# Two blocks of TensorE work moved ahead of the first flip of probabilities, in the local transformer of an adaLN network

## Chip, cores and metric

The kernel runs on one core of a Trainium2 chip. The metric is the time of one execution on the device in microseconds (us). Before the change the median of three runs is 4399.69 us (4398.7 to 4399.81).

## What is computed

The network has two layers, each with an attention part and a feed-forward part behind a modulated layer norm. Nearly all of the time goes into the feed-forward part of the first layer, which is itself a local transformer of six layers on 16 sequences of 256 tokens, width 128, with 16 heads of 64. Cut to what matters here, one of its layers is:

```python
def attn_layer(x, Wqkv, qs, ksc, Wo):
    q, k, v = jnp.split(x @ Wqkv, 3, -1)          # then split into heads
    q = l2norm(q) * qs
    k = l2norm(k) * ksc
    ...
    q = q * cos * scale + rotate_half(q) * sin * scale
    k = k * cos * inv + rotate_half(k) * sin * inv
    out = local_attention(q, k, v)                 # windows of 32 queries, 64 keys
    return out.transpose(0, 2, 1, 3).reshape(b, n, INNER) @ Wo

for i in range(DEPTH):
    x = attn_layer(shift_tokens(x), Wqkv[i], q_scale[i], k_scale[i], Wo[i]) + x
    x = ffn_layer(shift_tokens(x), ln_g[i], ln_b[i], W1[i], b1[i], W2[i], b2[i]) + x
```

`local_attention` multiplies each window of 32 queries with the 64 keys of its own and the preceding window, masks, takes a softmax, and multiplies with the values. `ffn_layer` is a layer norm, two matmuls with a gated GELU between them, and a matmul back.

## The kernel before

**Layout.** The state of two sequences (512 tokens) is one unit, kept as `z`, features on partitions. There are `NU = 8` units. A pair of heads fills 128 partitions, so a unit has `NP = 8` head pairs. Values and output projection are merged beforehand into one 128x128 matrix for each head (`wvo`), so that the "values" of the attention are the state itself.

**Steps.** The loop over `n` (lines 1009 to 1086) is one software pipeline over the six layers. A step takes two head pairs of one unit, `QS = 4` steps are a unit, 32 steps a layer, and 192 steps the stage, with nine more to drain. In one step stand stages of work of different head pairs:

- `project` (lines 633 to 661) multiplies the state with the weights of two head pairs (L648), squares the results on ScalarE (`sq`, L651), and forms the two halves of the rotary embedding on VectorE (L653, L656). The halves change places by DMA and are added by GpSimd one step later: four operations `rotate` (L664).
- `norms_sum` (lines 667 to 682), on even steps only, sums the squares of two steps over each head with the selector `sel`: 8 matmuls of 32 rows out (L672, 16 in the profile, which counts both passes of f32), and one copy `n2` on ScalarE (L681). `norms_inverse` turns the sums over and takes their inverse roots on GpSimd.
- `scaled` (L745) multiplies the keys with their inverse norms on GpSimd, twice in a step.
- `masked` (L771) writes the mask into two PSUM banks; `scores` (L793) adds 128 small products of queries and keys.
- `maxima` takes the row maxima `mx` (L805) and, in one small operation, the bias `nb` of the exponentials (L807), both on VectorE and once for each half `par` of the pair.
- `exponentials` (L815) are 16 activations on ScalarE for a step, in two groups of eight, `x = 0` and `x = 1`. The four operations `sq` of the same step's `project` stand between those of the first group: two exponentials, one `sq`, and so on. `divided` follows each group: a reciprocal (L828) and one product on GpSimd (`pr`, L830).
- `flipped` (L838), a step later, transposes the probabilities of one pair with four matmuls. The pair `x = 0` is copied out by ScalarE (L846), the pair `x = 1` by VectorE (L844), both into `prT`.
- `windows` (lines 747 to 764), on odd steps only, transposes the state of one sequence into the keys' view `xw`: eight matmuls (L755), one copy on ScalarE (L762), one on VectorE (L760), and one DMA that doubles it (L763).
- `weighted` (L856) multiplies state and probabilities, 8 matmuls (16 in the profile). In a step with `n % 4 == 0` it begins a unit and reads the `prT` that the two flips of the same step have just completed; in the other three it reads a `prT` completed earlier.
- `merging` (L877) multiplies with `wvo`, 32 matmuls in the profile. `ffn` is a generator that is advanced four times in a step.

With a unit of four steps, `ffn` always brings the same matmuls to the same place: the step with `n % 4 == 0` begins (after `merging`) with the last matmul of a unit's `ffn` (L962), the next with the variance (L912), the next with the gate (L939, GELU on ScalarE), and the last with the linear half (L949). Below they are called steps 0, 1, 2 and 3.

**What sets the order.** The region stands under a manual schedule for TensorE, VectorE, ScalarE and GpSimd: each executes its instructions in the order in which the Python code issues them. Four PSUM banks (`bank()`) are shared by everything but the scores and `merging`, each reused when its last reader is done.

Ahead of the change, the middle of a step is issued in this order:

```python
rotate(m, qs[m], got.pop(m))
...
flipped(p, 0, prs[n - 5], prTs[i, u])
...
    xws[v, s] = windows(v % NU, s)            # odd steps
sims = masked() if 0 <= n - 4 < N else None
...
flipped(p, 1, prs.pop(n - 5), prTs[i, u])
...
n2 = norms_sum([squares.pop(m) for m in range(2 * n - 4, 2 * n)])   # even steps
...
zxs[v, r] = weighted(r, xws[v, r // 2], prTs[v // NU, v % NU])
```

Of the kernel before, what the change touches and what calls it, by code (L numbers as in the profile page):

```python
# [19 lines left out]
NU = B // 2  # L20
U = 2 * L
DEPTH = 6
# [22 lines left out]
def adaln_kernel(  # L45
# [11 lines left out]
    def bank():  # L57
        return stage["ps"].tile([128, 512], F32, tag="mm", name="mm")

    def two(ap):  # L60
        return ap.rearrange("p (s t) -> p s t", s=2)
# [8 lines left out]
    def work(tag, shape=(128, 512), bufs=None):  # L70
        if stage.get("flat"):
            t = stage["flat"].tile([128, 512], F32, tag="flat", name=tag)
            if len(shape) == 4:
                t = t.rearrange("p (a b c) -> p a b c", a=shape[1], b=shape[2])
            return t
        kw = {} if bufs is None else {"bufs": bufs}
        return stage["pool"].tile(list(shape), F32, tag=tag, name=tag, **kw)
# [472 lines left out]
    with ExitStack() as es:  # L550
# [8 lines left out]
        def atile(tag, shape, bufs=None):  # L559
            kw = {} if bufs is None else {"bufs": bufs}  # L560
            return at.tile(list(shape), F32, tag=tag, name=tag, **kw)
# [29 lines left out]
        def load_ffn(i):  # L591
            w1 = wb.tile([128, 2 * FFH], F32, tag="w1", name="w1")
            nc.sync.dma_start(w1, io["L0_ffn_W1"][i])
            w2 = wb.tile([128, 3, D], F32, tag="w2", name="w2")
            nc.sync.dma_start(
                w2[:, 0:2, :],
                io["L0_ffn_W2"][i, 0:256, :].rearrange("(c k) d -> k c d", k=128),
            )
            nc.sync.dma_start(w2[0 : FFC[2], 2, :], io["L0_ffn_W2"][i, 256:FFH, :])
            return w1, w2  # L600
# [61 lines left out]
        def rotate(m, q, got):  # L662
            for j, r in enumerate((q, ks[m % 8][:, :, PAD:])):
                nc.gpsimd.tensor_tensor(r, r, two(got[:, j, :]), ALU.add)  # L664


        def norms_sum(squares):

            pn = bank()
            for odd in range(2):  # L670
                for g in range(4):
                    nc.tensor.matmul(  # L672
                        pn[32 * g : 32 * g + 32, :],
                        sel[:, odd, :],
                        squares[2 * (g % 2) + odd][1 - g // 2],
                        start=(odd == 0),
                        stop=(odd == 1),
                        skip_group_check=True,
                    )
            n2 = work("n2")  # L680
            nc.scalar.copy(n2, pn)  # L681
            return n2
# [59 lines left out]
        def scaled(m, kn):  # L742

            k = ks[m % 8][:, :, PAD:]
            nc.gpsimd.tensor_tensor(k, k, two(kn), ALU.mult)  # L745

        def windows(u, s):


            xw = atile("xw", (128, 8, 128))  # L750
            for g in range(2):
                pt = bank()
                for j in range(4):
                    w0 = 32 * (4 * g + j)
                    nc.tensor.transpose(  # L755
                        pt[0:64, j * 128 : (j + 1) * 128], zs[u][:, s, w0 : w0 + 64], ident
                    )
                dst = xw[0:64, 4 * g : 4 * g + 4, :].rearrange("p w d -> p (w d)")
                if g:
                    nc.vector.tensor_copy(dst, pt[0:64, :])  # L760
                else:
                    nc.scalar.copy(dst, pt[0:64, :])  # L762
            nc.sync.dma_start(xw[64:128], xw[0:64])  # L763
            return xw
# [207 lines left out]
        QS = NP // 2  # L972
        per = NU * QS
        N = DEPTH * per
# [3 lines left out]
        qs, squares, got, prs, prTs = {}, {}, {}, {}, {}  # L978
        xws, zxs, pys = {}, {}, {}
        inverses, kns = {}, {}  # L980
        n2 = rk = home = None
        behind, merges = [], []

        def place(n):

            return n // per, n % per // QS, 2 * (n % QS)
# [5 lines left out]
        def go_on(parts):  # L992
            for g in list(parts):
                if next(g, parts) is parts:
                    parts.remove(g)
# [12 lines left out]
        n = 0  # L1008
        while n < N + 9 or behind:
            layer, at_ = divmod(n, per)  # L1010
            if at_ == 13 and 0 < layer < DEPTH:
                wffs[layer] = load_ffn(layer)
            if 0 <= n - 4 < N:
                for m in (2 * (n - 4), 2 * (n - 4) + 1):
                    scaled(m, kns.pop(m))

            w, j = divmod(n - 9, QS)
            if 0 <= w < DEPTH * NU:
                if j == 0:
                    pys[w] = psy.tile([128, 512], F32, tag="y", name="y")  # L1020
                merging(j, zxs.pop((w, j)), vos[w // NU], pys[w])
                if j == QS - 1:
                    add_to_state(w % NU, pys.pop(w))
            if n % 2 and 3 <= n <= N + 1:
                home = norms_rows(rk)
            go_on(behind)
            go_on(merges)
            if 0 <= n - 1 < N:
                for m in (2 * (n - 1), 2 * (n - 1) + 1):
                    rotate(m, qs[m], got.pop(m))  # L1030
            if 0 <= n - 5 < N:
                i, u, p = place(n - 5)
                if p == 0:
                    prTs[i, u] = atile("prT", (128, NP, 512))
                flipped(p, 0, prs[n - 5], prTs[i, u])
            for s, lag in ((0, 7), (1, 9)):
                v, r = divmod(n - lag, QS)
                if r == 0 and 0 <= v < DEPTH * NU:
                    xws[v, s] = windows(v % NU, s)
            sims = masked() if 0 <= n - 4 < N else None  # L1040
            if 0 <= n - 5 < N:
                flipped(p, 1, prs.pop(n - 5), prTs[i, u])

            if n % 2 == 0 and 2 <= n <= N:
                n2 = norms_sum([squares.pop(m) for m in range(2 * n - 4, 2 * n)])
            v, r = divmod(n - 8, QS)
            if 0 <= v < DEPTH * NU:
                zxs[v, r] = weighted(r, xws[v, r // 2], prTs[v // NU, v % NU])
            go_on(behind)
            if sims:  # L1050
                m = 2 * (n - 4)
                rn = inverses[m // 4][:, m % 4 // 2]
                scores(sims, m, [qs.pop(m), qs.pop(m + 1)])
                pr = atile("pr", (128, 2, 4, 2, 64), 1)
                nbs = [maxima(sims[par], rn[:, par]) for par in range(2)]
                ssum = small("ssum", (128, 2, 4, 2))

            if n % 2 == 0 and 2 <= n <= N:
                rk, inverses[n // 2 - 1] = norms_inverse(n2)
            if 0 <= w < DEPTH * NU and j == QS - 1:  # L1060
                behind.append(ffn(w % NU, w // NU))
            go_on(behind)
            between = exponentials(0, sims, nbs, rn, pr, ssum) if sims else iter(())
            for m in (2 * n, 2 * n + 1):
                if n < N:
                    i, u, p = place(n)
                    qs[m], squares[m], got[m] = project(i, u, m, wqk[p + m % 2], between)
                if m % 2 == 0:
                    go_on(behind)
            if sims:  # L1070
                for x in range(2):
                    for _ in between:
                        pass
                    divided(pr[:, x], ssum[:, x])
                    between = exponentials(1, sims, nbs, rn, pr, ssum) if x == 0 else iter(())
                prs[n - 4] = pr
            if 0 <= n - 3 < N:
                for m in (2 * (n - 3), 2 * (n - 3) + 1):
                    kns[m] = widened(m, home)
            if layer + 1 < DEPTH:  # L1080
                if at_ == 18:
                    merges.append(merged(layer + 1))
                if at_ > per - QS:
                    p = 2 * (at_ - (per - QS) - 1)
                    wqk[p : p + 2] = [load_qk(layer + 1, p), load_qk(layer + 1, p + 1)]
            if at_ == 0 and 0 < layer < DEPTH:
                wqk[NP - 2 :] = [load_qk(layer, NP - 2), load_qk(layer, NP - 1)]
            n += 1
# [3 lines left out]
    for u in range(NU):  # L1092
        nc.sync.dma_start(xin[u], xhome[u])
        for hf in range(2):
            r, zv = zpart(u, hf)
# [13 lines left out]
    with ExitStack() as es:  # L1109
# [201 lines left out]
        N = len(steps)  # L1311
# [4 lines left out]
        n = 0  # L1316
        while n < N + 3 or running or merging:
# [12 lines left out]
            if n < N:  # L1330
                u, g, s, j = steps[n]
# [7 lines left out]
            if 0 <= n - 2 < N:  # L1339
                u, g, s, j = steps[n - 2]  # L1340
# [5 lines left out]
            if 0 <= n - 3 < N:  # L1346
                u, g, s, j = steps[n - 3]
# [116 lines left out]
```

## Time and profile before

One execution was profiled. It took 4399.63 us on the device, of which its span of instructions is 4397.6 us, with a mean granted TensorE clock of 0.964. The local transformer's pipeline runs from 396 us (its first waits) to 3765 us (its last `merging`).

| engine | busy in the span | us |
|---|---|---|
| TensorE, matmuls | 92% | 4060.0 |
| TensorE, weight loads | 60% | 2629.7 |
| VectorE | 64% | 2817.8 |
| ScalarE | 64% | 2829.9 |
| GpSimd | 59% | 2613.3 |

Four steps from the middle of the stage, each from the end of the last exponential of the step before to the end of its own, with the granted clock at 1.00 in each of the four windows:

| step | from, us | to, us | length, us | TensorE busy, us | ScalarE busy, us | GpSimd busy, us |
|---|---|---|---|---|---|---|
| 3 | 2007.30 | 2023.19 | 15.89 | 15.61 | 10.60 | 9.46 |
| 0 | 2023.19 | 2040.84 | 17.65 | 16.63 | 11.10 | 13.24 |
| 1 | 2040.84 | 2055.90 | 15.06 | 15.06 | 10.50 | 10.26 |
| 2 | 2055.90 | 2074.90 | 19.00 | 18.25 | 14.87 | 14.14 |

A timeline row gives the start, the duration, the engine (PE for matmuls, PEld for weight loads, DVE for VectorE, ACT for ScalarE, POOL for GpSimd), the line, the operation, the tiles it writes and reads, how many instructions are drawn together, and, in brackets, how long the engine was idle before it and what ended the wait. The ends of matmuls are modelled, so a busy TensorE is not one at its peak. In a group's row the first number behind the bar is the busy time in us, the second the mean of one in ns, and behind the second bar stands the idle time ahead of the group with those who ended it.

### The profile page before, as it was taken

The numbers are of one execution on the slowest core, as the hardware profiler recorded it, in microseconds if no ns is written. First come the engines' busy times: TensorE is split into PE (matmuls) and PEld (weight loads), VectorE is DVE, ScalarE is ACT, GpSimd is POOL, SyncE is SP. The second block draws the span as 40 slices with busy tenths as digits, with TensorE's granted clock in tenths as the row PEclk, the third lists the DMA queues.
The fourth block names the chain that finished last, engine by engine and source line by source line (L and its number), as shares of the span: only waits on it lengthen the run. The fifth ranks groups of instructions, "written<-read, shape, count | busy, mean of one in ns | idle before, by whom it ended". The sixth has DMA issues, their size and how long they took to land.

```text
span 4397.6 us, 118770 instructions
## 1 busy us (share of the span) xinstructions
PE 4060.0 (92%) x45721; PEld 2629.7 (60%) x45721; DVE 2817.8 (64%) x5987; ACT 2829.9 (64%) x9702; POOL 2613.3 (59%) x3302
## 2 busy tenths in 40 slices
PE   7667699999999999999999999999999998899998
PEld 4433466666666666666666666666666666545454
DVE  3434567777767777667676767767667675455554
ACT  3332567667676766767667676766767666477776
POOL 3323666676666676666766667666676764243432
PEclk7678899999999999999999999999999999999999
DMA  1022444444444444444444444444444442100000
GB/s 32 5 31 74 109 100 105 108 110 105 105 109 105 109 107 103 113 104 108 105 105 112 105 108 105 105 110 105 111 102 105 107 101 77 47 3 4 6 4 8
DMA packets 193548, 371.08 MB, mean 84 GB/s; under 512 B 42537, under 2 KB 83416, under 8 KB 192984
## 3 DMA queue, kind: packets, MB, share of 16 engines
q1 hardware_dynamic: 192984, 363.50, 33.5%
q8 instruction: 362, 5.93, 0.6%
q14 instruction: 202, 1.65, 0.1%
HBM read 127.92 MB, written 8.91 MB: 31 GB/s over the span
## 4 chain that ended last, share of the span: by engine, by line
PE 41%; DVE 20%; ACT 19%; POOL 5%; issue 5%; DMA 1%; SPq 0%; POOLq 0%; DVEq 0%; ACTq 0%
ACT pr L815 10%; PE mm L856 8%; PE sim L793 7%; DVE sent L653 5%; PE mm L672 4%; ACT sq L651 4%; PE mm L838 4%; POOL pr L830 4%; DVE k L656 3%; DVE q L656 3%; PE mm L648 3%; DVE mx L805 2%; PE mm L755 2%; PE mm L1251 2%; DVE nb L807 2%
## 5 line engine op out<-in xcount | busy, mean ns | idle before, releaser
L815 ACT ACTIVATE pr<-sim,nb,rq 128x64 f32<-128x64 f32 x3072 | 1229.5, 454 | 335.8 <-DVE nb L807 322.9
L830 POOL TENSOR_TENSOR pr<-pr,rsum 128x512 f32<-128x512 f32 x384 | 398.3, 1042 | 811.9 <-DVE rsum L828 776.8
L815 ACT ACTIVATION_READ_ACCUMULATOR pr<-sim,nb,rq 128x1 f32 x3072 | 784.9, 255 | 0.0
L877 PEld LDWEIGHTS y<-zx,wvo 128*128 128x128 f32 x6144 | 715.7, 192 | 91.5 <-issue 88.7
L877 PE MATMUL y<-zx,wvo 128*128 128x128 f32 x6144 | 717.5, 275 | 1.3 <-ACT zx L871 1.2
L648 PE MATMUL mm<-z,wqk 128*128 128x512 f32 x1536 | 705.1, 601 | 9.4 <-DMA wqk<-in_L_ffn_Wqkv_dram 7.2
L653 DVE SCALAR_TENSOR_TENSOR sent<-mm,vec,rope 128x512 f32<-128x512 f32 x768 | 569.9, 742 | 123.0 <-ACT sq L651 122.8
L651 ACT ACTIVATE sq<-mm 128x512 f32<-128x512 f32 x768 | 475.8, 620 | 33.6 <-PE mm L648 19.7
L664 POOL TENSOR_TENSOR k<-k,got 128x512 f32<-128x512 f32 x384 | 496.0, 1292 | 0.0
L664 POOL TENSOR_TENSOR q<-q,got 128x512 f32<-128x512 f32 x384 | 488.0, 1271 | 12.9 <-DMA got<-sent 9.8
L745 POOL TENSOR_TENSOR k<-k,kn 128x512 f32<-128x512 f32 x384 | 481.8, 1274 | 17.8 <-DMA kn<-rkh 17.8
L648 PEld LDWEIGHTS mm<-z,wqk 128*128 128x128 f32 x1536 | 278.7, 191 | 322.2 <-issue 236.4
L869 DVE COPY zx<-mm 128x512 f32<-128x512 f32 x384 | 265.4, 691 | 260.1 <-PE mm L856 260.0
L871 ACT COPY zx<-mm 128x512 f32<-128x512 f32 x384 | 224.8, 585 | 287.5 <-PE mm L856 287.5
L1224 POOL TENSOR_TENSOR pr<-pr,rsum 128x256 f32<-128x256 f32 (+1 forms) x256 | 206.1, 826 | 317.0 <-DVE rsum L1222 304.6
L856 PE MATMUL mm<-prT,xw 64*128 64x256 f32 x3072 | 390.0, 390 | 3.4 <-DVE zx L869 2.0
L805 DVE TENSOR_REDUCE mx<-sim 128x8 f32<-128x512 f32 x384 | 262.9, 685 | 172.3 <-PE sim L793 172.2
L856 PEld LDWEIGHTS mm<-prT,xw 64*128 64x128 f32 x3072 | 293.5, 187 | 122.3 <-issue 92.3
L838 PE MATMUL mm<-ident,pr 128*128 128x128 f32 x1536 | 245.3, 283 | 105.0 <-POOL pr L830 75.9
L838 PEld LDWEIGHTS mm<-ident,pr 128*128 128x128 f32 x1536 | 175.0, 142 | 270.1 <-POOL pr L830 240.6
L793 PEld LDWEIGHTS sim<-k,q 64*32 64x32 f32 x24576 | 265.7, 105 | 83.9 <-issue 56.8
L793 PE MATMUL sim<-k,q 64*32 64x64 f32 x24576 | 299.9, 226 | 16.6 <-issue 9.3
(236 smaller groups left out, 6649.2 us busy)
## 6 DMA issues: line engine op xcount, KB each, us to landing
got<-sent SPq DMA_DIRECT2D x1536, 128.0 KB
kn<-rkh SPq DMA_DIRECT2D x768, 128.0 KB
xw<-xw SPq DMA_DIRECT2D x96, 256.0 KB
wqk<-in_L_ffn_Wqkv_dram SPq DMA_DIRECT2D x48, 128.0 KB
bhome<-brow SPq DMA_DIRECT2D x1, 3072.0 KB
wv<-in_L_ffn_Wqkv_dram SPq DMA_DIRECT2D x12, 256.0 KB
wo<-in_L_ffn_Wo_dram SPq DMA_DIRECT2D x12, 256.0 KB
xt<-in_x_dram SPq DMA_DIRECT2D x8, 256.0 KB
```

Of the source, the lines that this page charges most:

```text
L648: nc.tensor.matmul(pp, wqk[:, j, :], xs, start=True, stop=True)
L651: nc.scalar.activation(sq, pp, AF.Square)
L653: nc.vector.scalar_tensor_tensor(two(sent[:, j, :]), two(pp), scale, tab[1], ALU.mult, ALU.mult)
L664: nc.gpsimd.tensor_tensor(r, r, two(got[:, j, :]), ALU.add)
L745: nc.gpsimd.tensor_tensor(k, k, two(kn), ALU.mult)
L793: nc.tensor.matmul(sims[par][32 * c : 32 * c + 32, c0 : c0 + 64], q[r, s, t0 : t0 + 32], k[r, s, t0 : t0 + 64], start=False, stop=True, sk ...
L805: nc.vector.tensor_reduce(mx, sim.rearrange("p (b k) -> p b k", b=8), AX.X, ALU.max)
L815: nc.scalar.activation(pr[:, x, st, par, :], sims[par][:, b * 64 : (b + 1) * 64], AF.Exp, bias=nbs[par][:, b : b + 1], scale=rn[:, par, b ...
L830: nc.gpsimd.tensor_tensor(prf, prf, rsum.unsqueeze(2).to_broadcast([128, 8, 64]), ALU.mult)
L838: nc.tensor.transpose(pt[:, st * 128 : (st + 1) * 128], pr[:, x, st].rearrange("p h k -> p (h k)"), ident,)
L856: nc.tensor.matmul(pz[par][:, w * 256 : (w + 1) * 256], xw[r, (2 * k + w) % 8, :], prT[r, :, 64 * k + 32 * w : 64 * k + 32 * w + 32], star ...
L877: nc.tensor.matmul(py[:, j * 128 : (j + 1) * 128], vo[:, h, :], zx[:, h % 2, h // 2, :], start=(h == 0), stop=(h == 2 * NP - 1), skip_grou ...
```

## The change

`norms_sum` (even steps) and `windows` (odd steps) are issued ahead of the first `flipped`, directly behind `rotate`, in place of behind the second and behind the first. Nothing is added or removed.

```diff
                 for m in (2 * (n - 1), 2 * (n - 1) + 1):
                     rotate(m, qs[m], got.pop(m))
+            if n % 2 == 0 and 2 <= n <= N:
+                n2 = norms_sum([squares.pop(m) for m in range(2 * n - 4, 2 * n)])
+            for s, lag in ((0, 7), (1, 9)):
+                v, r = divmod(n - lag, QS)
+                if r == 0 and 0 <= v < DEPTH * NU:
+                    xws[v, s] = windows(v % NU, s)
             if 0 <= n - 5 < N:
                 i, u, p = place(n - 5)
                 if p == 0:
                     prTs[i, u] = atile("prT", (128, NP, 512))
                 flipped(p, 0, prs[n - 5], prTs[i, u])
-            for s, lag in ((0, 7), (1, 9)):
-                v, r = divmod(n - lag, QS)
-                if r == 0 and 0 <= v < DEPTH * NU:
-                    xws[v, s] = windows(v % NU, s)
             sims = masked() if 0 <= n - 4 < N else None
             if 0 <= n - 5 < N:
                 flipped(p, 1, prs.pop(n - 5), prTs[i, u])
 
-            if n % 2 == 0 and 2 <= n <= N:
-                n2 = norms_sum([squares.pop(m) for m in range(2 * n - 4, 2 * n)])
             v, r = divmod(n - 8, QS)
```

In the built program the order on TensorE and ScalarE changes accordingly: in even steps L672 and its copy L681 now precede the first L838 and its copy L846, in odd steps L755 and its copy L762 do. The orders on VectorE and GpSimd are the same as before. The DMA queue of SyncE keeps its order but for the first few steps of the stage and one load of weights at each change of layer. PSUM banks are handed out in another order: in step 3 the first flip now takes the bank that the ScalarE copy of `windows` frees, and in step 2 the two flips take the first two banks that the GELU frees.

## The prediction

> **What bounds the kernel now.** I read the page first, then the waits of the flips (L838), then the timeline of four steps in a row, and last the operation `nb` (L807).
>
> ```profile
> PE 4060.0 (92%) x45721; PEld 2629.7 (60%) x45721; DVE 2817.8 (64%) x5987; ACT 2829.9 (64%) x9702; POOL 2613.3 (59%) x3302
> ...
> L838 PEld LDWEIGHTS mm<-ident,pr 128*128 128x128 f32 x1536 | 175.0, 142 | 270.1 <-POOL pr L830 240.6 <-POOL k L745 7.6 <-issue 5.2
> ```
>
> TensorE is the busiest engine, and its weight loads stand 240.6 us idle ahead of the flips until GpSimd has divided the probabilities. Together with the matmuls' own 75.9 us this is the gap that the moved work could fill. Whether filling it shortens a step depends on what starts the exponentials, since these are one unbroken chain on ScalarE: from the first to the end of the last 8.24 us in steps 1, 2 and 3 (2014.95 to 2023.19, for one) and 8.75 in step 0 (2032.09 to 2040.84).
>
> ```profile
> L807 DVE SCALAR_TENSOR_TENSOR nb<-mx,rq x384: 166/334/1308, 452.8 to 3718.5; 128x8 f32<-128x8 f32 x192
> ```
>
> This line of the view of `nb` (minimum, median, maximum in ns) shows an operation on 8 numbers a row that takes from 0.17 to 1.31 us. The timelines show why. Step 2:
>
> ```profile
> 2053.97 2.74 PE L939 MATMUL mm<-fx,w 128*128 128x512 f32 x6
> ...
> 2058.61 1.92 PE L672 MATMUL mm<-sq,sel 128*32 128x512 f32 x16
> ...
> 2063.98 1.26 POOL L664 TENSOR_TENSOR k<-k,got 128x512 f32<-128x512 f32 x1
> ...
> 2064.62 0.65 DVE L807 SCALAR_TENSOR_TENSOR nb<-mx,rq 128x8 f32<-128x8 f32 x1
> ...
> 2065.37 1.28 ACT L815 ACT_TABLE_LOAD   x1 [2.29 <-PE mm L648]
> ```
>
> `nb` begins at 2064.62 and ends at 2065.27, when the fourth rotation on GpSimd ends (2065.24). It is so in each of the four kinds of step: in step 0 it ends at 2031.97 and the rotation at 2031.95, in step 1 at 2047.55 and 2047.53, in step 3 at 2014.84 and 2014.81. The four rotations run without a gap, 1.24 us from one to the next, from a start that hangs on the exponentials before. So the next exponentials start on a grid of 1.24 us. TensorE decides only which tooth of it `nb` catches.
>
> **The even steps, step 2.** The block that moves is 16 matmuls. In issue it takes 1.85 us, from 2058.61 to the next matmul, L856, at 2060.46; the weights change from 128x32 to another split of the array, and each such change shows a pause of 0.09 us. Before, TensorE stood idle for most of the time between the end of L939 (its last issue at 2056.11, 0.43 for one of 512 columns, so 2056.54) and the sums. Now the sums start at 2056.54 + 0.09 = 2056.63, and the first flip at 2058.48; its probabilities have been ready since 2056.86, its bank (the first GELU) since 2057.83. From first flip to mask is 0.49 us (2056.91 to 2057.40), the mask 0.43, the second flip to `weighted` 0.53: `weighted` starts at 2059.94, against 2060.46. TensorE gains 0.52 us. The maxima, 3.43 us behind `weighted`, move along, and `nb` begins at 2064.10 in place of 2064.62. But the fourth rotation has started at 2063.98, 0.12 us earlier, and `nb` will end at 2065.27 as before. Gain: nothing.
>
> Here a rule and the trace are to be weighed. The Trainium skill, "Perfetto Trace Analysis", sections "Identifying the Most-Contended Engine" and "Optimization Strategy", says to find the gaps on the busiest engine and to make what they wait for come sooner. By it the 0.52 us would be gained, 40 times in the regular steps 2: 21 us. Another page, "SBUF — State Buffer", section "Who interferes with whom", speaks against: a VectorE operation with two SBUF inputs contends with a GpSimd operation that reads SBUF, and whichever comes second is fully blocked until the other ends. By that the gain is zero unless the start falls before 2063.98, and then 1.24 us at once. The ends of `nb` in all four steps are as the second rule has them, so I take zero.
>
> **Step 0.** Here the block was a cover.
>
> ```profile
> 2025.19 1.92 PE L672 MATMUL mm<-sq,sel 128*32 128x512 f32 x16
> ...
> 2026.25 0.69 DVE L844 COPY prT<-mm 128x512 f32<-128x512 f32 x1
> ...
> 2027.09 2.00 PE L856 MATMUL mm<-prT,xw 64*128 64x256 f32 x16
> ...
> 2031.25 0.72 DVE L807 SCALAR_TENSOR_TENSOR nb<-mx,rq 128x8 f32<-128x8 f32 x1
> ...
> 2031.78 3.60 PE L648 MATMUL mm<-z,wqk 128*128 128x512 f32 x8
> ...
> 2032.87 0.59 ACT L651 ACTIVATE sq<-mm 128x512 f32<-128x512 f32 x1
> ```
>
> `weighted` reads what the second flip has just delivered. The sums hid the copy of that flip (0.69 us, ended 2026.94) and were done at the same time as it. After the change nothing is between them. L962 gives TensorE free at 2023.33 in both versions (the idle time of TensorE ahead of both flips is only 0.24 us), so: sums at 2023.42, first flip 2025.27, mask 2025.76, second flip 2026.19, its copy 0.64 later (as 2042.42 to 2043.06 in step 1) at 2026.83 until 2027.52, `weighted` 0.12 to 0.15 later at 2027.67. That is 0.58 us late. VectorE is free for the copy (its work on `z` ends at 2026.22), so no more than that. From `weighted` on TensorE has no gap until `project` (L856, L793, L690, L903, L648), so all of it is 0.58 late.
>
> What waits for it: `nb` begins at 2031.83 and ends at 2032.00 (0.17 long, the rotation over at 2031.95), 0.03 us late, nearly free. The first exponentials are as good as on time. But the third operation on ScalarE is `sq` of the first product of `project`, whose second pass begins at 2032.21 and ends, with its modelled 0.59, at 2032.80; `sq` begins at 2032.87, with no slack. It now begins at 2033.43, and behind it in ScalarE's queue stand 14 exponentials, so the end of the step is 0.57 us late (0.58 less 0.02 of slack). What follows hangs on the exponentials and shifts alike. For the cost the ends are 0, if the copy did not hold up `weighted`, and 0.7, the whole copy; I take the worked 0.57.
>
> **Odd steps.** Step 1: TensorE waited 0.78 us for the first flip (until 2040.62), and now does `windows` (1.04 us by the row of L755) in that time, from 2039.85. The first flip then waits for its bank, which the ScalarE copy `rkT` frees at 2040.88, and the second flip for its probabilities (2042.20), as before; matmuls start at 2042.27 in place of 2042.42. `nb` began at 2047.37 and ends with the first rotation at 2047.53; 0.15 earlier changes nothing. Step 3: `windows` takes the bank that the first flip had (free 2007.33) and the flip takes the one freed by the ScalarE copy of `windows` (2008.72; before, the second half of `windows` waited for a copy until 2008.73). The two change places, and the mask starts at 2009.24 either way. Zero. ScalarE's copies change their order with the same number and length; the DMA of `xw` goes out up to 1 us sooner in step 1 and is waited for one step later. The copies of `windows` and of the sums need no other wait.
>
> **The sum.** Of the 44 steps 0 that have an L962 ahead of them, 34 are regular: 34 x 0.57 = 19.4 us. Ten stand next to the merging of weights for the next layer (L619, L628). In five of these TensorE comes to the flips late by its own work, and the copy costs up to 0.9; part falls on stalls within L793 that they have already, so 0.6 x 5 = 3.0. In the other five the second flip waited for a bank anyway and the sums fill that: -0.15 x 5 = -0.8. In five steps 2 next to them `nb` comes behind all rotations and gains some 0.3: -1.5. Together 20 us. Around the span lie 2.0 us in the profiled execution; 4397.6 + 2.0 + 20 = 4420, and its 4399.63 us is the median of the runs within 0.1 us.
>
> **The rivals.**
> - *Step 2 catches the tooth.* If TensorE gains 0.64 us or more, not 0.52, `nb` passes ahead of the fourth rotation: 1.24 x 40 = 50 us off, 4370, faster. It decides at 0.12 us, which is one pause and a bit; for it, that my start of the sums includes a pause that was not seen behind L939; against, that three such pauses stand in the new order and each was seen elsewhere.
> - *Step 0's lateness is absorbed*, by a shorter drain into `weighted`, or in L793, which has stalls of its own in some of these steps: 4400, the same.
> - *An odd step misses its tooth.* In step 3 `nb` begins 0.16 us before the fourth rotation (2014.60, 2014.76). If the exchanged banks make it later by that, it ends 1.24 us later, 40 times: 50 more, 4470.
> - *All gaps filled*: 316.5 us off, 4083. The grid excludes it.
>
> **How the numbers follow.** The forecast 0.66 (its own range 4411 to 4430), the caught tooth 0.10, absorbed 0.12, missed tooth 0.08, others 0.04. The range 4396 to 4440 holds the first and the third case and leaves out the two teeth, 0.18. A difference under 0.2% (8.8 us) is about what a measurement of this kernel can't tell from none. Slower: 0.66 + 0.08 + 0.02 = 0.76; same 0.12; faster 0.12.
>
> **What would show it.** In step 0 `weighted` starts some 4.45 us behind the last exponential, not 3.86, and ScalarE is idle 0.5 us before the first `sq`; idle time ahead of L651 grows from 33.6 by about 20 us. In step 2 `nb` starts 0.5 us sooner, lasts 1.17 us and ends as before. The flips' waits for GpSimd fall to a third or less, for nothing. Steps 1 and 3 keep 15.06 and 15.89. I am wrong if step 2 is not 19.0 us long, or step 0 not 18.2.

## The result, and the profile after

The changed kernel takes 4423.57 us (median of four runs, 4421.47 to 4426.57), the kernel before 4399.65 us (four runs, 4398.7 to 4399.81). The ratio is 1.0055, with a 95% interval of 1.0038 to 1.0073: slower, by 23.9 us in the medians. The profiled execution is the slowest of the four: it took 4426.57 us, of which 4424.6 are its span, at a mean granted TensorE clock of 0.969.

The rows of the changed kernel that answer to those shown of before, from the page and from the groups of instructions by line:

```profile
span 4424.6 us, 119003 instructions
PE 4080.1 (92%) x45721; PEld 2629.7 (59%) x45721; DVE 2830.1 (64%) x5987; ACT 2833.0 (64%) x9702; POOL 2612.4 (59%) x3302
...
L651 ACT ACTIVATE sq<-mm 128x512 f32<-128x512 f32 x768 | 474.6, 618 | 42.4 <-PE mm L648 28.5
```

```profile
L838 PEld LDWEIGHTS mm<-ident,pr 128*128 128x128 f32 x1536 | 175.0, 142 | 185.3 <-POOL pr L830 143.0 <-POOL k L745 8.1 <-issue 6.8
...
L856 PE MATMUL mm<-prT,xw 64*128 64x256 f32 x3072 | 397.1, 391 | 48.1 <-DVE prT L844 44.2 <-DVE zx L869 3.9
```

Before the change the rows of the squares (L651) and of `weighted` (L856) were these:

```profile
L651 ACT ACTIVATE sq<-mm 128x512 f32<-128x512 f32 x768 | 475.8, 620 | 33.6 <-PE mm L648 19.7 <-DMA wqk<-in_L_ffn_Wqkv_dram 13.9
L856 PE MATMUL mm<-prT,xw 64*128 64x256 f32 x3072 | 390.0, 390 | 3.4 <-DVE zx L869 2.0 <-DVE prT L844 1.4
```

The gap that the moved work was to fill did shrink: the weight loads of the flips stand 143.0 us idle for GpSimd's probabilities, where it was 240.6. But TensorE has a new wait: `weighted` (L856) waits 44.2 us for VectorE's copy of the second flip, where it waited 1.4 before. And the squares (L651) wait 28.5 us for TensorE's product, where it was 19.7.

Where that went is told by the kinds of step. Each length runs from the end of the last exponential (E) of the step before to the end of its own; the times of `weighted` (its first weight load) and of `nb` count from E. Steps are numbered by `n`. All lengths and times are medians over some 45 steps, before and after:

| step | length, us | `weighted` starts | first `nb` starts | first `nb` ends | sum over the steps from the 16th on, us |
|---|---|---|---|---|---|
| 0 | 17.65, 18.32 | 3.86, 4.45 | 8.05, 8.73 | 8.78, 8.90 | +26.1 |
| 1 | 15.07, 15.09 | 2.11, 2.00 | 6.52, 6.39 | 6.71, 6.72 | +3.3 |
| 2 | 19.00, 18.99 | 4.55, 4.02 | 8.71, 8.18 | 9.36, 9.35 | -0.6 |
| 3 | 15.89, 15.91 | 2.90, 2.90 | 7.28, 7.28 | 7.54, 7.54 | +4.3 |

The last column is the sum of the differences in length. It comes to +33.1; the eleven steps before the 16th are 6.6 us shorter in all; together with what lies around the pipeline (+0.5) that is the 27.0 us by which the two spans differ.

The timeline of a step 2 of the changed kernel (E at 2270.61):

```profile
2271.33 1.92 PE L672 MATMUL mm<-sq,sel 128*32 128x512 f32 x16
...
2274.64 2.00 PE L856 MATMUL mm<-prT,xw 64*128 64x256 f32 x16
...
2278.66 1.27 POOL L664 TENSOR_TENSOR k<-k,got 128x512 f32<-128x512 f32 x1
2278.80 1.17 DVE L807 SCALAR_TENSOR_TENSOR nb<-mx,rq 128x8 f32<-128x8 f32 x1
2280.06 1.28 ACT L815 ACT_TABLE_LOAD   x1 [2.81 <-DVE nb L807]
```

The sums start 0.72 us behind E, and `weighted` at E + 4.03, half a microsecond sooner than before. `nb` begins 0.14 us behind the fourth rotation and ends at 2279.97, 0.04 us behind the rotation's end (2279.93). It now lasts 1.17 us for 8 numbers a row, and the exponentials start when they did.

The timeline of the step 0 that follows two steps later (E at 2305.50):

```profile
2305.67 1.92 PE L672 MATMUL mm<-sq,sel 128*32 128x512 f32 x16
...
2309.09 0.69 DVE L844 COPY prT<-mm 128x512 f32<-128x512 f32 x1 [0.56 <-PE mm L838]
...
2309.93 2.12 PE L856 MATMUL mm<-prT,xw 64*128 64x256 f32 x16 [0.87 <-DVE prT L844]
...
2314.21 0.17 DVE L807 SCALAR_TENSOR_TENSOR nb<-mx,rq 128x8 f32<-128x8 f32 x1
...
2314.74 3.60 PE L648 MATMUL mm<-z,wqk 128*128 128x512 f32 x8
...
2315.80 0.60 ACT L651 ACTIVATE sq<-mm 128x512 f32<-128x512 f32 x1 [0.43 <-PE mm L648]
```

TensorE stands 0.87 us idle ahead of `weighted`, for the copy that the sums had covered, and ScalarE 0.43 us ahead of the first square, for a product that comes late.

### The profile page after: what moved, and what is told of

It reads as the page before. It is cut to its first block, busy times and chain, and to the rows that moved or that the text cites. A ratio compares the mean times of both kernels' runs of the same rounds, so it can differ in the third digit from the quotient of the medians.

```text
span 4424.6 us, 119003 instructions
## 1 busy us (share of the span) xinstructions
PE 4080.1 (92%) x45721; PEld 2629.7 (59%) x45721; DVE 2830.1 (64%) x5987; ACT 2833.0 (64%) x9702; POOL 2612.4 (59%) x3302
## 4 chain that ended last, share of the span: by engine, by line
PE 55%; ACT 18%; DVE 11%; issue 3%; POOL 3%; DMA 1%; SPq 0%; POOLq 0%; ACTq 0%; DVEq 0%
ACT pr L815 9%; PE mm L856 8%; PE mm L648 8%; PE y L877 7%; PE sim L793 6%; PE mm L838 4%; ACT sq L651 4%; PE mm L672 3%; PE mm L939 3%; PE mm L962 2%; POOL pr L830 2%; PE mm L1251 2%; DVE sent L653 2%; DVE nb L807 2%; PE sim L1188 2%
## 5 line engine op out<-in xcount | busy, mean ns | idle before, releaser
L815 ACT ACTIVATION_READ_ACCUMULATOR pr<-sim,nb,rq 128x1 f32 x3072 | 771.4, 251 | 0.0
L653 DVE SCALAR_TENSOR_TENSOR sent<-mm,vec,rope 128x512 f32<-128x512 f32 x768 | 570.7, 743 | 133.4 <-ACT sq L651 126.2
L651 ACT ACTIVATE sq<-mm 128x512 f32<-128x512 f32 x768 | 474.6, 618 | 42.4 <-PE mm L648 28.5
L856 PE MATMUL mm<-prT,xw 64*128 64x256 f32 x3072 | 397.1, 391 | 48.1 <-DVE prT L844 44.2
L856 PEld LDWEIGHTS mm<-prT,xw 64*128 64x128 f32 x3072 | 300.7, 188 | 103.8 <-issue 69.9
L793 PE MATMUL sim<-k,q 64*32 64x64 f32 x24576 | 301.8, 227 | 20.8 <-issue 10.3
L793 PEld LDWEIGHTS sim<-k,q 64*32 64x32 f32 x24576 | 266.2, 105 | 87.8 <-issue 49.0
L844 DVE COPY prT<-mm 128x512 f32<-128x512 f32 x192 | 132.8, 692 | 287.0 <-PE mm L838 286.9
L1213 ACT ACTIVATE pr<-lg,nm 128x128 f32<-128x128 f32 (+1 forms) x512 | 226.5, 444 | 93.7 <-DVE nm L1202 82.0
```

The source lines that it names most:

```text
L651: nc.scalar.activation(sq, pp, AF.Square)
L653: nc.vector.scalar_tensor_tensor(two(sent[:, j, :]), two(pp), scale, tab[1], ALU.mult, ALU.mult)
L793: nc.tensor.matmul(sims[par][32 * c : 32 * c + 32, c0 : c0 + 64], q[r, s, t0 : t0 + 32], k[r, s, t0 : t0 + 64], start=False, stop=True, sk ...
L815: nc.scalar.activation(pr[:, x, st, par, :], sims[par][:, b * 64 : (b + 1) * 64], AF.Exp, bias=nbs[par][:, b : b + 1], scale=rn[:, par, b ...
L856: nc.tensor.matmul(pz[par][:, w * 256 : (w + 1) * 256], xw[r, (2 * k + w) % 8, :], prT[r, :, 64 * k + 32 * w : 64 * k + 32 * w + 32], star ...
```

## The experiments

The theory to be tested has three parts: the loss is step 0's alone and reaches the time through the first square; in step 2 the start gained is taken by the rotations on GpSimd; the odd steps neither gain nor lose. The kernels of before run beside the experiments had medians of 4395.93 (with the first three), 4396.64 (with the next four), 4398.23 (with the three after) and 4394.69 us (with the last two). In what follows E and the lengths are as in the table above.

### Each part of the change alone

The first moves the sums in steps 0 only, the second in steps 2 only; the diff of the first is

```diff
+            if n % 4 == 0 and 2 <= n <= N:
+                n2 = norms_sum([squares.pop(m) for m in range(2 * n - 4, 2 * n)])
             if 0 <= n - 5 < N:
...
-            if n % 2 == 0 and 2 <= n <= N:
+            if n % 4 == 2 and 2 <= n <= N:
                 n2 = norms_sum([squares.pop(m) for m in range(2 * n - 4, 2 * n)])
```

and the second has 2 and 0 exchanged. The third moves the block of `windows` alone.

> Only the sums of squares of step 0 (n % 4 == 0) move ahead of the first flip; those of step 2 and the keys' view stay. If the loss is the uncovered copy of step 0's second flip: about +0.64 us in each regular step 0 (the median that the profile after shows), 34 of them, and little at the layer changes: 4421 to 4427, step 2 as before with its matmuls at the old places. If the loss came from the move as a whole (banks, DMA order, instruction fetch): clearly under half of the 24 us.

> Only the sums of step 2 (n % 4 == 2) move. By the grid of GpSimd's rotations: TensorE gets to its scores 0.53 us sooner in some 40 steps, nb waits it out (1.17 us long in place of 0.65), the time stays within 4 us of 4400. If gaps of TensorE counted: 40 x 0.53 = 21 us off, 4379.

> Only the keys' view of odd steps moves. Its matmuls fill TensorE's wait of step 1, the rest of the step is held by the probabilities and by the first tooth of the rotations: 4400, within 5 us; steps 1 and 3 keep 15.07 and 15.90 in the median. If it had a share in the loss: 4405 or more.

| moved | time, us | ratio to before, 95% interval | what the step shows |
|---|---|---|---|
| sums, steps 0 | 4420.28 | 1.0060 (1.0043 to 1.0076) | step 0 18.37, `weighted` at 4.45 |
| sums, steps 2 | 4393.84 | 0.9997 (0.9988 to 1.0005) | step 2 18.99, `weighted` at 4.03, `nb` 8.20 to 9.36 |
| keys' view, odd steps | 4400.66 | 1.0010 (1.0003 to 1.0017) | steps 1 and 3 at 15.07 and 15.89 in the median |

The whole loss stands in the first row, at a time just under the expected 4421 to 4427. The second row has TensorE 0.52 us earlier in the median step 2 and no gain. The third has a loss of a tenth of a per cent. Its steps 1 are 4.1 us longer in their sum with no change in their median, so single steps lost, and not each a little: in one (`n` = 189) `nb` missed a tooth and ends at 7.94 in place of 6.71, and in three (57, 93 and 165) `nb` is on time, but the first square waits 0.48 to 0.95 us for its product.

### Is it the grid of rotations that takes the gain of step 2?

If it is, the rotations set the time, and pushing them *later* by a small useless operation on GpSimd should make the kernel with the sums moved in step 2 *faster*, since `nb` then comes ahead of the fourth rotation. In the kernel before the same operation should only cost time.

```diff
+            if n % 4 == 2 and 5 < n < N:
+                nc.gpsimd.tensor_tensor(
+                    small("idle", (128, 64), 2), ident[:, 0:64], ident[:, 64:128], ALU.add
+                )
             if 0 <= n - 1 < N:
                 for m in (2 * (n - 1), 2 * (n - 1) + 1):
                     rotate(m, qs[m], got.pop(m))
```

> As the kernel that moves only the sums of step 2, and GpSimd gets one useless addition (128x64, some 0.32 us) ahead of the rotations of every step 2. By the grid: the rotations start about 0.35 us later, the fourth then begins behind nb (0.12 us was missing), nb passes between the third and the fourth, and step 2 is about 0.9 us shorter: 36 us off, 4364. If the place of the rotations doesn't matter, or added work only costs: 4400 or more.

> The kernel before with the same useless addition on GpSimd in every step 2 and nothing moved. By the grid nb (which begins 0.63 us behind the fourth rotation's old start) still falls into the fourth rotation, which now ends 0.35 us later: 40 x 0.35 = 14 us more, 4414. If added work on an engine that is busy 59% of the time is hidden: 4400.

With the sums moved in steps 2: 4362.84 us, ratio 0.9925 (0.9910 to 0.9940). In the kernel before: 4407.39 us, ratio 1.0026 (1.0015 to 1.0037). The timeline of a step 2 of the first of these (E at 2306.02):

```profile
2310.38 0.34 POOL L1029 TENSOR_TENSOR idle<-ident 128x64 f32<-128x64 f32 x1
...
2313.11 1.29 POOL L664 TENSOR_TENSOR q<-q,got 128x512 f32<-128x512 f32 x1
2314.21 0.22 DVE L807 SCALAR_TENSOR_TENSOR nb<-mx,rq 128x8 f32<-128x8 f32 x1
2314.34 1.30 POOL L664 TENSOR_TENSOR k<-k,got 128x512 f32<-128x512 f32 x1
```

`nb` starts where it did (E + 8.19), but now 0.13 us ahead of the fourth rotation, and ends with the third, at 2314.43. The step is 18.05 us long, not 18.99. In the kernel before, the useless operation cost 10.8 us. With the sums moved, which alone had made no difference, it left the kernel 33.8 us under the kernel before. In the kernel before, the end of `nb` moved by 0.29 us (9.36 to 9.65), a little less than expected, and so did the time (4414 was expected).

### Taking the contention away

The Trainium skill, "SBUF — State Buffer", section "Who interferes with whom", says that a VectorE operation with at most one input in SBUF (outside its faster modes) does not contend with GpSimd. That can be had here without a new instruction: the maxima are written to a PSUM bank, and `nb` reads them there.

```diff
-        def maxima(sim, rn):
+        def maxima(sim, rn, mx):
-            mx = small("mx", (128, 8))
             nc.vector.tensor_reduce(mx, sim.rearrange("p (b k) -> p b k", b=8), AX.X, ALU.max)
...
-                nbs = [maxima(sims[par], rn[:, par]) for par in range(2)]
+                pm = bank()
+                nbs = [maxima(sims[par], rn[:, par], pm[:, 8 * par : 8 * par + 8]) for par in range(2)]
```

> The order of the kernel before; the row maxima are written to a PSUM bank, so that nb has one input in SBUF in place of two. If nb waits because its second SBUF input meets a rotation that reads SBUF: nb lasts 0.2 us everywhere, step 2 is 0.48 us shorter, step 3 0.08, step 0 not (its first square waits for its product): 42 x 0.56 = 24 us off, 4376. If nb waits for something else in GpSimd: 4400, with nb as long as before.

> Maxima in PSUM, and the sums of step 2 moved. Without the grid the 0.53 us of TensorE in step 2 count: 0.48 + 0.53 + 0.08 us in 42 rounds of four steps, 45 us off, 4354, faster than either kernel. If the move of step 2 gains nothing even then: 4376, as with the maxima in PSUM alone.

In the kernel before: 4367.71 us, ratio 0.9938 (0.9923 to 0.9953). With the sums moved in steps 2 as well: 4350.76 us, ratio 0.9897 (0.9881 to 0.9914). The view of `nb` with the maxima in PSUM (minimum, median, maximum in ns):

```profile
L806 DVE SCALAR_TENSOR_TENSOR nb<-mm,rq x384: 165/167/168, 450.7 to 3685.7; 128x8 f32<-128x8 f32 x192
```

All 384 now last the same, which agrees with the rule. Both kernels are somewhat faster than expected (4376 and 4354). The edit also takes one more bank and writes the maxima to another place, so the 28.9 us by which the first falls are those of the whole edit. Step 2 falls to 18.58, and with its sums moved to 18.10: the 0.5 us that TensorE gains there is worth something once `nb` isn't bound to the grid. Step 0 stays at 17.64, although its first exponential starts 0.5 us sooner (8.40): the first square now waits for its product. That is the wait which the change lengthens.

### Does step 0's loss run through the first square?

If so, two more exponentials ahead of that square should fill its wait and bring the changed kernel back to the time of before. The same edit in the kernel before is the control.

```diff
                 next(between, None)
+                if j == 0 and m % 8 == 0:
+                    next(between, None)
                 sq = work("sq")
```

> The changed kernel, but in a step 0 four exponentials instead of two stand on ScalarE ahead of the first square. Theory (the lateness of TensorE reaches the time only through the first square, which waits 0.43 us for its product): two exponentials fill that wait, the first exponential starts as in the changed kernel (9.01 us behind the last of the step before), and step 0 falls from 18.3 to 17.8 or 17.9, so 18 to 20 us off: 4400 to 4406. Rival (the late stage of weighted delays something else too, the maxima or a later product): step 0 stays at 18.2 or more, 4418 to 4424.

> The kernel before with the same two exponentials ahead of the first square of a step 0, as the control. Theory: there the square waits for nothing (0.07 us), so nothing is gained: step 0 stays at 17.6 or 17.7, 4394 to 4400. Rival (the order of exponentials and squares is worth something by itself): a step 0 shorter by 0.2 us or more, 4390 or less.

The changed kernel with it: 4407.4 us, ratio 1.0021 (1.0015 to 1.0028), somewhat over the 4400 to 4406 expected. Step 0 is 17.86 us, with `weighted` as late as in the changed kernel (4.45) and the first exponential at 9.04. From the first exponential to the last a step 0 takes 8.77 us, as in the kernel before (8.76), where the changed kernel takes 9.31. So most of the lateness did cost through the first square. What is left, 0.2 us a step, is for the most part the later start of the first exponential (9.04, before 8.89). Summed over the steps 0 only 2.7 us of the 26.1 are left, but the control, below, wins 9.9 us in its own steps 0, and against it 12.6 us are left. In the steps 1 this kernel is 7.0 us above the kernel before, where the changed one was 3.3; of this the control tells, too. The wait is the 0.43 us in brackets in the changed kernel's timeline above; in this kernel the bracket is gone:

```profile
2306.27 3.60 PE L648 MATMUL mm<-z,wqk 128*128 128x512 f32 x8
...
2307.56 0.60 ACT L653 ACTIVATE sq<-mm 128x512 f32<-128x512 f32 x1
```

The control did not do what was expected: 4453.77 us, ratio 1.0126 (1.0111 to 1.0141), where both theories had it at 4400 or less. Step 0 is as long as before in the median (17.66). In their sum the steps 0 are 9.9 us shorter: in the kernel before, 15 of 44 had waited for the product of the first square, 9.0 us in all, and now 0.1 us is left of that. But step 1 went from 15.07 to 16.45. Timelines of the step 1 that follows, of the kernel before (E at 2311.27):

```profile
2309.59 0.19 DVE L828 RECIPROCAL rsum<-ssum 128x8 f32<-128x8 f32 x1
...
2311.05 0.66 PE L838 MATMUL mm<-ident,pr 128*128 128x128 f32 x4 [0.79 <-POOL pr L830]
...
2317.75 0.23 DVE L807 SCALAR_TENSOR_TENSOR nb<-mx,rq 128x8 f32<-128x8 f32 x1
```

and of the control (E at 2337.50; all lines are two further down in its code):

```profile
2336.59 0.19 DVE L830 RECIPROCAL rsum<-ssum 128x8 f32<-128x8 f32 x1
...
2338.05 0.66 PE L840 MATMUL mm<-ident,pr 128*128 128x128 f32 x4 [1.56 <-POOL pr L832]
...
2344.76 0.81 DVE L809 SCALAR_TENSOR_TENSOR nb<-mx,rq 128x8 f32<-128x8 f32 x1
```

VectorE's halves of the rotary embedding wait for the squares (in the kernel before 122.8 us of idle time ahead of L653 are ended by L651), and the first reciprocal stands behind them in VectorE's queue. With later squares it starts 0.91 us ahead of E, not 1.68. The first flip of step 1 moves by the same 0.77 us (from E - 0.22 to E + 0.55), and `weighted` with it (2.11 to 2.87). The second rotation begins at 2344.29 and takes 1.26 us; `nb` starts at 2344.76, behind that begin, and ends at 2345.57, with the rotation. In the kernel before it ended with the first. A step 1 has lost a tooth. In the changed kernel with the later square a step 1 is only 0.16 us longer than in the kernel before, with the first flip just as late (E + 0.55) and `weighted` at 2.14. There `windows`, moved ahead of the first flip, gives TensorE work for the wait. So the second half of the change may have a use after all, where the first flip is late; the last kernels below try it.

### Putting the parts together

First the maxima in PSUM, the sums moved in steps 2 and the later square in steps 0:

> Row maxima in PSUM, sums of squares ahead in steps 2 only, and four exponentials ahead of the first square of a step 0. Without the last the first exponential of a step 0 started at 8.40 us, 0.5 us sooner than in the kernel before, and the square then waited for its product. Theory: the wait is filled, step 0 falls from 17.6 to 17.2, 40 times 0.45 = 18 us off the 4351 of the kernel without it: 4333. Rival (step 0 is then held by its later products or by what divides the probabilities): 4345 to 4351.

4363.75 us, ratio 0.9921 (0.9904 to 0.9937): worse than without the square, outside of both expectations. Step 0 fell to 17.17 as expected, but step 1 went to 15.87, by the wait that the control had shown (`weighted` at 2.88). The last two kernels add the moved keys' view, with and without the later square:

> The kernel before with four parts: row maxima in PSUM, sums of squares ahead in steps 2 only, four exponentials ahead of the first square of a step 0, and the keys' view ahead of the first flip in odd steps, as the change has it. Without the last it took 4363.75 us, with weighted in a step 1 at 2.88 and the step 15.87 long. Theory (the later squares delay VectorE's halves and with them the first reciprocal, by 0.77 us; the first flip of step 1 waits for the probabilities behind it; the keys' view, 1.04 us of TensorE, fills that wait): weighted in a step 1 at 2.1 to 2.2, the step 15.1 to 15.2, 45 times 0.7 = 32 us off: 4332. Rival (the lateness reaches the maxima on another way, by GpSimd's scaled keys behind the divided probabilities): step 1 stays at 15.8, 4360 to 4365.

> The same without the exponentials ahead of the square: row maxima in PSUM, sums of squares ahead in steps 2 only, keys' view ahead in odd steps. Theory (without a late first flip the keys' view has nothing to fill that counts): step 1 gains at most the 0.1 us by which weighted starts sooner, now that no rotation holds nb to a grid: 4346 to 4352, against 4350.76 without the keys' view. Rival (the view is worth its 1.04 us of waiting once nb is free of the grid): 4320 or less.

With the square: 4329.68 us (4327.5 to 4330.56), ratio 0.9848 (0.9832 to 0.9865). Without it: 4347.66 us, ratio 0.9890 (0.9876 to 0.9905). The steps in the median:

| maxima in PSUM, sums moved in steps 2, and | step 0 | step 1 | step 2 | step 3 | time, us |
|---|---|---|---|---|---|
| nothing | 17.64 | 15.11 | 18.10 | 15.87 | 4350.76 |
| later square | 17.17 | 15.87 | 18.10 | 15.88 | 4363.75 |
| keys' view | 17.64 | 14.99 | 18.10 | 15.86 | 4347.66 |
| later square, keys' view | 17.16 | 15.01 | 18.18 | 15.87 | 4329.68 |

The keys' view alone makes no difference that these runs can tell (the intervals 0.9881 to 0.9914 and 0.9876 to 0.9905 overlap). Where the later square has made the first flip of step 1 late, it is worth 34.1 us in the medians, or 32 us by the ratios to the kernels of before beside them (0.9921 and 0.9848). The last row is the fastest kernel found: 1.5% under the kernel before, and by the two ratios to it (0.9848 / 1.0055) 2.1% under the changed one.

## Why the prediction was right, and where it was off

The forecast was 4420 us, and it came out at 4423.57, within the likeliest case's own range. The two kinds of step on which the argument rests behaved as it said. The sum is nearer than its terms. Measured are the differences of the two profiled executions, whose spans differ by 27.0 us; the first three rows count from the 16th step on:

| term | forecast, us | measured, us |
|---|---|---|
| steps 0 | 19.4 + 3.0 - 0.8 = 21.6 | 26.1 |
| steps 2 | -1.5 | -0.6 |
| odd steps | 0 | 7.6 |
| the eleven steps before the 16th | 0 | -6.6 |
| around the pipeline | 0 | 0.5 |

That the fourth row nearly pays for the third is luck.

- **Step 2, gain nothing: right, and shown.** TensorE gained 0.53 us (predicted 0.52), `nb` began 0.53 sooner and lasted 1.16 in the median (predicted 1.17). It missed the fourth rotation by 0.14 us (predicted 0.12). Moving the rotations and taking the contention away both set the gain free, so the cause is the rotations and not something else that ends at the same time. The rule of filling the gaps of the busiest engine, which would have had 21 us here, gave 0.9997 of the time before in the kernel that moved only this.
- **Step 0, +0.57: right in its mechanism, somewhat small.** `weighted` is late by 0.59 (predicted 0.58), and the first square waits. The regular step itself is 0.64 to 0.67 longer. The term left out is `weighted`'s own stretch: from its start to the scores' it takes 2.04 us in the median, where it took 1.96. What lengthens it was not tried, and stays open. The first exponentials, taken as good as on time (0.03 us), start 0.12 us later. They cost nothing as long as the square waits anyway, and are most of what is left once it does not. Over the 35 regular steps from the 16th on the sum is 22.0 us; 18 of them lost between 0.55 and 0.75 us, and the others lie between -1.3 and +2.3.
- **The stalls within the scores (L793) make much of that spread.** The prediction named them, but not what they hang on. From the 16th step on the kernel before has 12 pauses of over 0.2 us between two products of a step's scores, and the changed kernel 17, together 11.9 and 14.2 us. The trace shows no wait that ends them. Counted over all of TensorE's recorded instructions (matmuls, weight loads and semaphore waits), every one of them stands at the same place, to within one instruction, of a block of 256. It is so in all 14 profiled kernels, 163 pauses, all of them among the last 34 of a step's 128 products. So where they fall follows from how many instructions stand ahead, and a change in the order moves them: the profile has 1483 semaphore waits of TensorE after the change, and 1251 before. Why TensorE pauses there, and why at some of these places only, is not shown.
- **The edges: wrong in size, and two in sign.** The five steps 0 in which TensorE comes late were to lose 0.6 each; one of them lost 1.95, the others between -0.06 and +0.33. The second five were to gain 0.15; three changed by some 0.05, and two lost 0.6. The five steps 2 beside them were to gain 0.3 and lost 0.29.
- **Odd steps, zero: right for the median, not for the sum.** With 15.09 and 15.91 they are within 0.02 us of the lengths of before, but single steps missed a tooth (three steps 1 and three steps 3 are 1.24 us longer each, and one step 1 is 1.1 shorter). With the small shifts of the others that is 7.6 us. In all six the scores had one of the stalls just told: they took 1.89 to 2.44 us, where they took 1.56 to 1.62 in the same steps before. The rival in which *every* step 3 misses its tooth did not come. That a margin of 0.16 us is now and then used up by a stall was left out of the sum.
- **The start of the pipeline was taken at nothing and gave 6.6 us.** Three of the first steps (`n` = 7, 10 and 12) are 2.0 to 2.7 us shorter each. In these same steps the mean granted clock was 0.70, 0.91 and 0.91 in the profiled execution before, and 0.93, 1.00 and 1.00 in the one after. That the change brought this is not shown: over the 14 profiled executions the time at half clock in these eleven steps lies anywhere between 18.5 and 35.3 us (32.3 before, 22.0 after).
- **What was to show it.** ScalarE's idle time ahead of the squares grew from 33.6 to 42.4, by 9 and not by 20. Ahead of the first square of a step 0 it was 9.0 us before, in 15 of the 44 steps, and is 18.8 now, in 40. So a third of these steps had the wait already, and there it did not grow (6.1 us now); the others have 12.8 us of it. A regular one shows 0.43 us and not 0.55, because the first exponentials start 0.12 us later too (the end of `nb`, 8.78 and 8.90). The flips' waits for GpSimd's `pr` halved, over matmuls and weight loads together (316.5 us to 163.3), where a third or less was predicted.

## What to carry to other kernels

Before filling a gap on the busiest engine, follow the work behind it to what starts the next stage: here a 0.17 us operation on VectorE was bound to the rhythm of another engine, and half a microsecond won ahead of it 40 times was worth nothing until that bond was cut (one operand in PSUM). A block that stands between a producer and its consumer may be the cover of a copy; moving it ahead costs the copy. And try parts of a change again after the bound has moved: the keys' view was worth nothing, or a tenth of a per cent less than nothing, in the kernel before, and some 32 us where the first flip was late.

## What the runs showed of the hardware that had not been expected

- With a useless operation of some 0.3 us on GpSimd in 47 steps a kernel was 0.75% faster than the kernel before where the sums were moved, and 0.26% slower where they weren't.
- `nb` gets between two rotations that are recorded as following one another without a gap. It did where it began 0.13 us ahead of the next rotation's start, and it did not where it began 0.14 us behind it. Its end was then 0.03 to 0.04 us behind a rotation's end.
- With one input in PSUM the same operation takes 165 to 168 ns in all 384 executions, where it took up to 1308 before. The Trainium skill, "SBUF — State Buffer", section "Who interferes with whom", states the rule for VectorE operations in general; here the edit that follows it was worth 29 us.
- A wait on ScalarE can be paid for on VectorE and TensorE a step later: two exponentials moved ahead of one square cost 55.5 us (4453.77 against 4398.23), because VectorE's work on a product waits for ScalarE's square of it (122.8 us of idle time in the kernel before), and the reciprocals wait behind that work.
- TensorE's unexplained pauses within the scores, 0.2 to 1.9 us each, stand at one place of every 256 of its recorded instructions, in all 163 cases. They move when instructions ahead of them are added or reordered, and six of them cost a tooth of the grid here.
